# A sparse graph layer and a masked attention layer: rows put in order of their neighbour count on the chip

## The chip, the cores and the metric

The kernel runs on one core of a Trainium2 chip. The core has five engines that the text names by their short forms: PE (TensorE, matrix products), DVE (VectorE), ACT (ScalarE), POOL (GpSimd) and SP (SyncE, which only issues DMAs here). The time is that of the device, in microseconds (us): 2217.14 us for the kernel before, the median of 3 runs (2214.53 to 2218.22).

## The reference

`x` holds 8 graphs of 2048 rows with 256 features, and `adj` is one weighted 2048 x 2048 adjacency matrix that all graphs share. It is sparse: row `n` is linked to row `m` with a chance that falls as `1/sqrt((1+n)(1+m))`, so the first rows have many neighbours and the last ones few. Every row is linked to itself.

```
# layer 0: graph convolution, two linear layers with batch norm
A_norm = adj + eye;  deg = sum(A_norm, 0) + sum(A_norm, 1) - diag(A_norm)
agg = (A_norm * rsqrt(deg)[:, None] * rsqrt(deg)[None, :]) @ x
h   = relu(batchnorm(agg @ W1.T + b1));  y = batchnorm(h @ W2.T + b2)
x   = layernorm(x + y)
# layer 1: attention with 4 heads of 64, masked to the neighbours
q, k, v = split(x @ W)
o   = softmax(q k^T / 8 where adj != 0) v
x   = layernorm(x + o)
```

## The kernel before

The 2048 rows are cut into 16 blocks of 128 rows, one row to a partition. Block 0 holds the rows with the most neighbours and is worked on as a dense block; the others use lists of neighbours.

**The search** (`search_steps`, L214). For each row the kernel turns the non-zero places of its adjacency row into numbers that fall with the column (L219) and takes the eight largest at a time over all 2048 columns (MAX8, L223), striking out what it found (L226), in 2 to 4 rounds. `list_steps` (L231) then makes the list of block `t`: `LISTS[t] = (r, cap)` means that each row keeps its first `r` neighbours in `r` aligned slots ("tiles" of 128 rows with one neighbour each), and what is left over in the block is packed into `cap` further tiles, through one-hot matrices built on DVE (L262, L265) and products on PE (L272). All blocks have 132 tiles together, 40 of them such left-over tiles.

**Stage A, loading** (L387 to L439). The 16 blocks of `adj` are loaded into 16 buffers ("slots", `Slot`, 1 MB each, which every later stage up to the attention shares). ACT sums the rows, PE the columns, POOL takes the power of -1/2 (`rsqrt`, L136).

**Stage B, dense** (L444 to L467). `x` is loaded, scaled and written to `xs_d`, one DRAM row of 8 KB for each node with all 8 graphs. Blocks 0 and 1 (`DENSE = 2`) are multiplied as dense matrices while it passes (L454).

**Stage C, sparse** (L512 to L627). For each of the 116 tiles of blocks 2 to 15, POOL issues two gathers through an index list ("indirect DMA"[...]): 4 bytes from `adj` for the weights (`gather_value`, L311, 16 tiles ahead) and 8 KB a row from `xs_d` (L524, up to 8 tiles ahead). A tile is then added up on DVE (L593 for the first of a block, L597 for the others) or, with a diagonal or one-hot matrix as weights, on PE (L606). The rest of the search and of the lists runs between the tiles. A finished block is transposed (L371) and multiplied with W1 (L489), and the result goes to `h_d`.

**Stage D, second linear layer** (L636 to L785). 16 pairs of 512-column pieces go through a Strassen-like scheme with 7 products instead of 8; POOL makes its four differences for each pair (`form`, L685, L694).

**Stage E, attention** (L856 to L1342). Two graphs are worked on at once, so there are four passes over the 132 tiles. A pass is prepared by 8 `projection` units, which load `y` and `x`, normalise, and write keys with values (`kv_d`) and queries (`q_d`) to DRAM. The units of the first pass stand alone ("the run-in"); those of the following passes lie between the tiles of the pass before. For each tile POOL gathers keys and values (`kg`, L1192, ten tiles ahead), for a left-over tile also the queries (`qg`, L1198); DVE multiplies and sums (L1210, L1212), ACT takes the exponential (L1221), DVE or ACT weigh the values (L1241, L1236), PE adds up (L1252). `finish` (L1062) divides on DVE, `residual` (L1070) adds to `x` on POOL, and the row is normalised and stored by SP (L1106).

All order is written by hand: each engine takes its instructions in the order in which the program emits them, and `at(n, f, ...)` puts a step of a unit behind tile `n`. POOL's queue holds its arithmetic and all gathers, SP's the plain loads and stores.

## Time and profile before

| what | us |
|---|---|
| median of 3 runs | 2217.14 |
| the profiled execution, its own time | 2243.83 |
| its span, from the first to the last instruction | 2242.0 |
| stage A: loading, to the first product of stage B | 0 to 73 |
| stage B: dense | 73 to 187 |
| stage C: sparse, to the end of the W1 products | 187 to 622 |
| stage D: last W1 products, then the 16 pairs from 664 | 622 to 846 |
| stage E: run-in, to the first tile | 846 to 996 |
| stage E: four passes of 132 tiles | 996 to 2218 |
| end | 2218 to 2242 |

The stages are read from the chain of work that ended last and from the lists of instructions by time. In a row of a group of instructions, "busy" is the sum of the durations (overlaps counted once), then the mean of one in ns, then the time the engine stood idle just before them and what ended it. "issue" is idle time in which nothing the profile shows was waited for. In a table by stretches each engine has its busy time and its number of instructions, and then come the granted PE clock, the share of the 16 DMA engines and the rate of the DMAs.

### The profile page before, as it was taken

To read this page: it belongs to the slowest core of one execution; us is meant where nothing else is said; L and a number is where in the kernel's file an instruction comes from. 1 tells how busy PE (TensorE), PEld (TensorE's weight loads), DVE (VectorE), ACT (ScalarE), POOL (GpSimd) and SP (SyncE) were. 2 spreads that over 40 slices of the span, in tenths; PEclk is the share of its full clock that TensorE was granted. 3 is DMA by queue.
4 is the path that set the end of the run, shared out by engine and by line. 5 is a ranking of instruction groups with operands and counts; after the bars stand their busy time and mean duration, and the time that the engine had idled before them with its cause. 6 is when DMAs were issued, how large, how long until landed. Compare 5 with 4: busy or idle time off the path is not lost.

```text
span 2242.0 us, 27795 instructions
## 1 busy us (share of the span) xinstructions
PE 1989.4 (89%) x7720; PEld 1285.6 (57%) x7720; DVE 1824.6 (81%) x3461; ACT 1303.6 (58%) x3896; POOL 1445.7 (64%) x1443
## 2 busy tenths in 40 slices
PE   5899797899999997979999999999999999678884
PEld 1444344454444444647777777777777776566663
DVE  6897999798556663239999999899988999978996
ACT  6331132233354544647777777777777777678875
POOL 2504778886048771136777787768876778878884
PEclk7899898999999998989999999999999999889896
DMA  8887999899567625569898999999999999999994
GB/s 317 282 300 290 369 339 367 317 424 370 210 247 285 231 85 204 194 247 340 301 368 325 346 356 357 343 324 375 330 363 350 333 359 337 349 357 339 334 350 151
DMA packets 232628, 698.67 MB, mean 312 GB/s; under 512 B 24976, under 2 KB 91280, under 8 KB 206352
## 3 DMA queue, kind: packets, MB, share of 16 engines
q0 software_dynamic: 109248, 442.68, 52.9%
q1 hardware_dynamic: 120912, 237.34, 29.1%
q10 hardware_dynamic: 2304, 16.78, 1.8%
q8 instruction: 64, 1.05, 0.2%
q14 instruction: 100, 0.82, 0.1%
HBM read 565.91 MB, written 130.81 MB: 311 GB/s over the span
## 4 chain that ended last, share of the span: by engine, by line
PE 44%; DVE 26%; issue 9%; DMA 8%; ACT 7%; POOL 6%; another core or an unknown queue 0%; SPq 0%; DVEq 0%; POOLq 0%; ACTq 0%
PE pm L977 9%; PE pa L699 8%; PE po L1252 7%; DVE pr L1210 7%; PE pa L454 5%; PE ph L489 5%; DVE wv L1241 4%; ACT wv L1236 3%; DVE s L1212 3%; DMA e<-xs_d,idx 3%; POOL kg L1192 2%; PE pa L606 2%; DMA e<-in_adj_dram 2%; PE po L1045 2%; DVE e L597 2%
## 5 line engine op out<-in xcount | busy, mean ns | idle before, releaser
L1192 POOL DMA_INDIRECT kg<-kv_d,idx x528 | 567.6, 1075 | 159.4 <-issue 103.4
L1236 ACT ACTIVATE wv<-kg,pw 128x65 f32<-128x65 f32 x1896 | 477.6, 337 | 8.8 <-PE po L1045 3.8
L1252 PE MATMUL po<-wv,ident 128*128 128x260 f32 x1472 | 421.2, 399 | 51.4 <-DVE z L1066 39.1
L1212 DVE TENSOR_REDUCE s<-pr 128x8 f32<-128x512 f32 x528 | 362.1, 686 | 34.7 <-DVE pr L1210 0.5
L977 PE MATMUL pm<-wq,x1t 128*128 128x512 f32 (+1 forms) x1024 | 374.8, 496 | 12.6 <-ACT x1t L922 10.0
L1252 PEld LDWEIGHTS po<-wv,ident 128*128 128x128 f32 x1472 | 277.9, 198 | 122.2 <-issue 66.9
L1221 ACT ACTIVATE pw<-s,padb 128x8 f32<-128x8 f32 x528 | 157.2, 299 | 201.4 <-DVE s L1212 161.4
L1210 DVE TENSOR_TENSOR pr<-qb,kg 128x512 f32<-128x512 f32 x368 | 260.2, 707 | 4.0 <-issue 1.0
L977 PEld LDWEIGHTS pm<-wq,x1t 128*128 128x128 f32 x1024 | 186.1, 192 | 103.7 <-issue 73.7
L524 POOL DMA_INDIRECT e<-xs_d,idx x116 | 148.3, 1279 | 140.5 <-DMA xs_d<-xt 66.1
L1241 DVE TENSOR_TENSOR wv<-kg,pw 128x520 f32<-128x520 f32 x291 | 211.0, 725 | 16.8 <-PE po L1252 5.7
L1252 PE MATMUL po<-wv,oh 128*128 128x260 f32 x640 | 196.6, 398 | 7.8 <-DVE wv L1241 6.5
L489 PE MATMUL ph<-e,w1s 128*128 128x512 f32 x448 | 197.4, 593 | 0.0
L1198 POOL DMA_INDIRECT qg<-q_d,idxq x160 | 164.6, 1029 | 48.8 <-issue 47.9
L311 POOL DMA_INDIRECT av<-in_adj_dram,fidx x116 | 162.3, 1399 | 45.8 <-issue 32.3
L493 ACT ACTIVATE h<-ph,b1s 128x512 f32<-128x512 f32 x112 | 76.9, 687 | 181.1 <-PE ph L489 171.2
L606 PE MATMUL pa<-e,wt 128*128 128x512 f32 x352 | 166.9, 622 | 12.3 <-DVE wgt L323 4.6
L1045 PEld LDWEIGHTS po<-kvr,p 128*128 128x128 f32 x1024 | 138.9, 199 | 37.1 <-ACT p L1034 13.3
L1045 PE MATMUL po<-kvr,p 128*128 128x65 f32 x1024 | 136.0, 278 | 21.4 <-ACT p L1034 9.8
L1026 PE MATMUL pm<-q,kt 128*128 128x256 f32 x512 | 140.7, 400 | 13.1 <-POOL q L929 9.8
L597 DVE SCALAR_TENSOR_TENSOR e<-e,wgt,e 128x2048 f32<-128x2048 f32 x58 | 135.9, 2343 | 9.2 <-DMA e<-xs_d,idx 6.2
L1252 PEld LDWEIGHTS po<-wv,oh 128*128 128x128 f32 x640 | 120.4, 199 | 37.9 <-issue 15.8
(192 smaller groups left out, 3352.0 us busy)
## 6 DMA issues: line engine op xcount, KB each, us to landing
kv_d<-kvr SPq DMA_DIRECT2D x32, 1032.0 KB
h_d<-h SPq DMA_DIRECT2D x28, 1024.0 KB
e<-h_d SPq DMA_DIRECT2D x28, 1024.0 KB
e<-in_adj_dram SPq DMA_DIRECT2D x16, 1024.0 KB
xt<-in_x_dram SPq DMA_DIRECT2D x16, 1024.0 KB
xs_d<-xt ACTq DMA_DIRECT2D x16, 1024.0 KB
y_d<-y SPq DMA_DIRECT2D x32, 512.0 KB
yt<-y_d SPq DMA_DIRECT2D x32, 512.0 KB
```

What stands on the lines that cost most here:

```text
L489: nc.tensor.matmul(ph, w1s[:, d, f * P : (f + 1) * P], v[:, d, b, :], start=(d == 0), stop=(d == ND - 1),)
L597: nc.vector.scalar_tensor_tensor(agr[t].t, xg[n].t, wgt[:, col : col + 1], agr[t].t, op0=ALU.mult, op1=ALU.add,)
L606: nc.tensor.matmul(pa[c], w, xg[n].t[:, c * CH : (c + 1) * CH], start=(k == 0), stop=(k == count - 1),)
L699: nc.tensor.matmul(py, w[:, f, :], t[:, f, :], start=(f == 0), stop=(f == 1))
L977: nc.tensor.matmul(pm, x1t[b, c][:, d, i * P : (i + 1) * P], rhs(d), start=(d == 0), stop=(d == ND - 1),)
L1045: nc.tensor.matmul(po0[b][:, h, :], p[:, h, :], heads(kvr[b, c][:, i, D:])[:, h, :], start=(j == 0 and h == 0), stop=(j == NT - 1), skip_g ...
L1192: nc.gpsimd.indirect_dma_start(out=kg[n].rearrange("p b e -> p (b e)"), out_offset=None, in_=kv_d[p][:], in_offset=bass.IndirectOffsetOnAx ...
L1210: nc.vector.tensor_mul(pr, q, kg[n][:, :, :D])
L1212: nc.vector.tensor_reduce(s.rearrange("p b h -> p (b h)"), pr.rearrange("p b (h e) -> p (b h) e", e=HD), AX.X, ALU.add,)
L1236: nc.scalar.activation(wv[n][:, b, hs], k[:, b, D:][:, hs], AF.Copy, scale=w[:, b, h : h + 1],)
L1241: nc.vector.tensor_mul(wv[n].rearrange("p b (h e) -> p b h e", e=VW), k[:, :, D:].rearrange("p b (h e) -> p b h e", e=VW), w[:, :, :, None ...
L1252: nc.tensor.matmul(po[p, t, b].rearrange("p h e -> p (h e)"), oh[n] if e >= 0 else ident, wv[n][:, b, :], start=(r == 0), stop=(r == ELL[t ...
```

## The change

Each row's number of neighbours is counted, and the rows are ranked by it on the chip: rank 0 is the row with the most neighbours. Row `n` gets its place `pos[n]`; the 2048 places are again cut into 16 blocks. Rows of one block now have nearly the same number of neighbours, so block `t` has `DEPTH[t]` aligned tiles and no left-over tiles, and the last tiles of a block hold only the rows that still have a neighbour (`FEWER`, partial tiles of 4 to 120 rows). There are 125 tiles instead of 132 (14,988 rows instead of 16,896).

- **Search** (`search`): MAX8 runs on 16 segments of 8 to 248 columns and then on the 128 candidates. ACT counts neighbours (a second pass over each block). Ten blocks are searched before the ranking, six after it. The search is over before stage C.
- **Records**: a row's list, number, degree factor and count are written as one 128-byte record to its place in `rec_d` by an indirect DMA for each block (`hand_over`), and read back in order. `pos` is written to `pos_d`.
- **Dense**: only block 0 (the 128 rows with the most neighbours, gathered into `hubs`) is dense; block 1 is sparse as well. The tiles of a block are shared by DVE and PE as `ON_TENSOR` says (28 on PE, 97 on DVE).
- **Stage C**: before the first tile POOL issues 7 value gathers, 10 row gathers, 17 value gathers and `own_rows`. Between the tiles POOL also issues `lookups`: because keys and values are stored in order of rank, each of the 125 index lists is translated through `pos_d` by a 4-byte indirect DMA (62 in stage C, 32 in stage D, 31 in the run-in), and 16 scatters of the mask of block 0.
- **Stage E**: `x` rows are gathered by index (128 indirect DMAs on POOL instead of 32 loads on SP), output rows are scattered by index (128 indirect DMAs on POOL instead of 34 stores on SP), no queries are gathered and no one-hot tiles are made, and `finish` adds to `x` itself, in four instructions on DVE, so that `residual` is gone.

```diff
+DEPTH = (0, 19, 14, 12, 11, 9, 9, 8, 7, 7, 6, 6, 5, 5, 4, 3)
+GROUPS = ((0, 1, 8, 13), (2, 6, 12, 15), (3, 5, 10, 14), (4, 7, 9, 11))
+TURN = (0, 15, 14, 13, 1, 12, 2, 11, 3, 10, 4, 9, 5, 6, 7, 8)
+ON_TENSOR = (0, 6, 4, 3, 3, 2, 2, 2, 2, 2, 1, 1, 0, 0, 0, 0)
...
+    def search(t):
+        s = rows_of.pop(t)
+        a = s.t
+        nc.vector.scalar_tensor_tensor(a, a, 0.0, down, op0=ALU.not_equal, op1=ALU.mult)
+        best = lists.tile([P, 8 * (len(SEGMENTS) - 1)], F32, name="best", bufs=2)
+        for i, (u, v) in enumerate(zip(SEGMENTS, SEGMENTS[1:])):
+            nc.vector.max(out=best[:, 8 * i : 8 * i + 8], in_=a[:, u:v])
+        s.done()
+        for r in range(MAXNB // 8):
+            m8 = own[:, t, 8 * r : 8 * r + 8]
+            nc.vector.max(out=m8, in_=best)
+            if r + 1 < MAXNB // 8:
+                nc.vector.match_replace(out=best, in_to_replace=m8, in_values=best, imm_value=0.0)
...
+    def hand_over(t):
+        nc.vector.tensor_tensor(
+            own[:, t, MISS : MISS + 1], found[:, t : t + 1], count[:, t : t + 1],
+            op=ALU.not_equal,
+        )
+        spill(rec_d[:], posi[:, t : t + 1], own[:, t, :])
...
+                nc.scalar.activation(junk, a, AF.Sign, accum_out=count[:, t : t + 1])
...
+            for t in range(AHEAD_OF_RANK):
+                search(t)
...
+            nc.gpsimd.dma_start(pos_d.rearrange("(t p) o -> p (t o)", p=P), posi)
...
+            hubs = Slot()
+            pick(hubs.t, adj[:, :], hubi)
+            for t in range(AHEAD_OF_RANK, NT):
+                search(t)
+            for t in range(NT):
+                hand_over(t)
...
+        nc.sync.dma_start(rec, rec_d.rearrange("(t p) e -> p t e", p=P))
...
+        VLEAD, START = 24, 7
+        for n in range(START):
+            gather_value(n)
         gather_ahead(0)
+        for n in range(START, VLEAD):
+            gather_value(n)
+        own_rows = Slot()
+        pick(own_rows.t, xs_d[:], hubi)
+        nc.vector.scalar_tensor_tensor(
+            agr[0].t, own_rows.t, row_scale(0), agr[0].t, op0=ALU.mult, op1=ALU.add
+        )
...
         for n in range(len(tiles)):
...
+            v = n + VLEAD
+            if v < len(tiles):
+                gather_value(v)
...
+            if n % 2:
+                next(lookups, None)
+            if n % 7 == 3 and n // 7 < NT:
+                m = n // 7
+                spill(bias_d[:], posi[:, m : m + 1], masks[:, m, :])
...
             gather_ahead(n + 1)
...
             second_linear(n)
+            for _ in range(2):
+                next(lookups, None)
...
+            def load_rows(b, c, i):
+                t = GROUPS[c][i]
+                pick(x1[b, c][:, i, :], x_rows, idr[:, b, t : t + 1])
...
             def finish(b, t, po):
+                c, i = place[t]
                 ri = inv_all[:, b, t, :]
                 nc.vector.reciprocal(ri, po[:, :, HD])
-                z = zs[b, t] = ip.tile([P, D], F32, name="z", bufs=4)
-                nc.vector.tensor_mul(
-                    heads(z), po[:, :, :HD], ri[:, :, None].to_broadcast([P, NHEADS, HD])
-                )
-
-            def residual(b, t):
-                c, i = divmod(t, TPC)
-                to = rest[b] if late(b, t) else x1[b, c]
-                nc.gpsimd.tensor_add(to[:, i, :], zs.pop((b, t)), to[:, i, :])
+                to = heads((rest[b] if late(b, t) else x1[b, c])[:, i, :])
+                for h in range(NHEADS):
+                    nc.vector.scalar_tensor_tensor(
+                        to[:, h, :], po[:, h, :HD], ri[:, h : h + 1], to[:, h, :],
+                        op0=ALU.mult, op1=ALU.add,
+                    )
...
+            def put(b, c, i):
+                t = GROUPS[c][i]
+                spill(out_rows, idr[:, b, t : t + 1], x1[b, c][:, i, :])
...
             for n in range(min(later), 0):
                 side_tasks(n)
+                next(lookups, None)
```

`pick` is an indirect DMA that gathers rows by an index list, `spill` one that scatters them; both are issued by POOL.

## The prediction

> **What bounds the kernel now.** I read the stretches first, one for each stage (stage E at one pass), to see who is busy in each.
>
> ```profile
> core 0: us, PE busy (x) PEld busy (x) DVE busy (x) ACT busy (x) POOL busy (x), PEclk, DMA share, GB/s
> 73.00:187.00 114.00, 112.66 (x257) 49.61 (x258) 97.25 (x77) 28.78 (x17) 29.09 (x28) 0.98 0.83 290
> 187.00:272.00 85.00, 73.57 (x222) 36.04 (x223) 83.99 (x133) 10.31 (x23) 59.09 (x48) 0.97 0.87 346
> 272.00:450.00 178.00, 156.47 (x442) 78.28 (x441) 156.37 (x318) 45.58 (x71) 137.98 (x97) 0.91 0.90 339
> 450.00:622.00 172.00, 166.57 (x486) 80.64 (x484) 135.04 (x232) 59.11 (x93) 83.19 (x59) 0.98 0.81 327
> 664.00:846.00 182.00, 180.56 (x421) 79.73 (x420) 118.02 (x174) 81.81 (x119) 138.76 (x60) 1.00 0.52 196
> 846.00:963.00 117.00, 101.62 (x392) 64.76 (x392) 34.86 (x108) 67.82 (x162) 14.13 (x56) 0.93 0.56 191
> ...
> 1301.00:1606.00 305.00, 285.00 (x1356) 218.99 (x1355) 283.40 (x587) 230.33 (x789) 232.22 (x264) 0.98 0.94 347
> ```
>
> PE fills stages B and D. Stage C is held by DVE up to 272 (84 of 85 us, search and lists) and then by PE. In a pass of stage E, PE and DVE share the limit, 285 and 283 of 305 us. POOL looks free. The second view, the groups, says what one piece of its work costs.
>
> ```profile
> L1192 POOL DMA_INDIRECT kg<-kv_d,idx x528 | 567.6, 1075 | 159.4 <-issue 103.4
> L524 POOL DMA_INDIRECT e<-xs_d,idx x116 | 148.3, 1279 | 140.5 <-DMA xs_d<-xt 66.1
> L1198 POOL DMA_INDIRECT qg<-q_d,idxq x160 | 164.6, 1029 | 48.8 <-issue 47.9
> L311 POOL DMA_INDIRECT av<-in_adj_dram,fidx x116 | 162.3, 1399 | 45.8 <-issue 32.3
> L489 PE MATMUL ph<-e,w1s 128*128 128x512 f32 x448 | 197.4, 593 | 0.0
> L606 PE MATMUL pa<-e,wt 128*128 128x512 f32 x352 | 166.9, 622 | 12.3 <-DVE wgt L323 4.6
> L597 DVE SCALAR_TENSOR_TENSOR e<-e,wgt,e 128x2048 f32<-128x2048 f32 x58 | 135.9, 2343 | 9.2 <-DMA e<-xs_d,idx 6.2
> ```
>
> A 4-byte gather costs POOL no less than one of 8 KB a row. Why their means differ from the commonest duration, 0.94 us, shows in order of time:
>
> ```profile
> 199.30 2.29 DVE L223 MAX8 nbx<-e 128x8 f32<-128x2048 f32 x1
> ...
> 200.50 0.93 POOL L524 DMA_INDIRECT e<-xs_d,idx  x1 [0.30 <-issue]
> ...
> 324.52 2.34 DVE L597 SCALAR_TENSOR_TENSOR e<-e,wgt,e 128x2048 f32<-128x2048 f32 x1
> 324.95 2.73 POOL L311 DMA_INDIRECT av<-in_adj_dram,fidx  x1 [0.30 <-issue]
> ...
> 327.99 0.94 POOL L524 DMA_INDIRECT e<-xs_d,idx  x1 [0.30 <-issue]
> 329.14 2.34 DVE L597 SCALAR_TENSOR_TENSOR e<-e,wgt,e 128x2048 f32<-128x2048 f32 x1
> 329.23 3.07 POOL L311 DMA_INDIRECT av<-in_adj_dram,fidx  x1 [0.31 <-issue]
> ```
>
> A gather that starts under a multiply-add of DVE ends 0.82 us after it (326.86 to 327.68, 331.48 to 332.30); one under MAX8 is not held. With 0.30 us of issue behind each, a gather occupies POOL 1.24 us, plus what it is held.
>
> **Before the sparse stage.** ACT reads each block twice: its 2.45 us per block become 4.45, so the counts end near 5.9+71 = 77. A search is one pass (2.29, L219), 16 MAX8 over 2048 columns in all (2.13 by the 2.29 row; 0.06 to 0.16 more for each, I take 0.11: 3.9) and 1.9 for the 128 candidates: 8.1 us. Ten, from 10.4 on, end at 91. Ranking and its round trips to PE and POOL, some 13, the list of hubs, 9 (16 products at 0.55): 113. POOL's plain DMA of 4-byte places stands ahead of the degree factor; from 1 us to 15 (2048 descriptors at POOL's 0.94 for 128), I take 2, in the 13. Six searches, 49: 162. Then POOL has 16 records, 20 us: 182; landing, reading back and index arithmetic 8: **190** (175 to 205). One dense block, 128 products of 0.44 = 56 us on PE, from about 123 to 179, and the passage of `x` lie under this. So the list is ready when stage C begins now, and stages A and B gain nothing: what leaves stage C (search and one-hot lists on DVE) goes ahead of it.
>
> **The sparse stage.** DVE: 15 first tiles at 1.28, 82 multiply-adds at 2.3, 11 blocks of `add_rows` (44 at 0.74), 120 statistics at 0.69, small ones 10: some 335 us. PE: 28 tiles of 3.44, 480 W1 products of 0.43, transposes 32: 335. At the 0.93 that PE and DVE reach elsewhere that is 360, against 435 now. But POOL:
> - At the opening, 35 indirect DMAs before and with `own_rows`: 43 us, and its landing 4. DVE waits for it; the weights and all multiply-adds are queued behind that, and PE's transposes and ACT's diagonal matrices wait for those. Start: **238**.
> - Then up to the last row gather: 101 values, 57 lookups, 16 masks, 115 rows = 289 at 1.24 = 358 us.
> - Held: now 39.8+52.7 us beyond 0.94 in the two groups, over some 70 two-input passes (58 of L597, 12 of the search), 1.3 each with POOL occupied 77% of the time, so 1.7 at full occupation (2.34 less half a gather is 1.72; back to back it is 1.1). I take 1.6 for 74 of them: 118.
> - Partial tiles: 18 with 72 rows on average. The trace has none; their cost lies between no saving and one in proportion (0.41 x 45 = 18). I take 9.
>
> Here the GPSIMD Engine Reference of the Trainium skill (Key points) goes further than the row: contention comes from DVE instructions with two SBUF inputs, which the rows show, *and* from those in a 2-port mode. The first-tile pass (1.28 us for 2048) is such a one; no gather starts under one here, so the rule would add up to 14 x 0.65 = 9 us. I leave it out, as the rows are silent.
>
> Sum 467 from 233: the last row gather at 700, last tile and transposes 15, last W1 products 14 (32 x 0.435, half of now), run-in of stage D 21.5 as now: its pairs start at 751 instead of 664, **+87**.
>
> **Second linear layer.** POOL has 4 x 2.36 a pair and 2 lookups, 11.9 us against PE's 11.2; over 14 pairs it falls back 10, of which its lead covers about half: **+5** (0 to 12). The 512-byte stores of `y` go to DMA engines half idle: 0.
>
> **Run-in.** POOL, almost idle now, takes 4 row gathers a unit and a lookup at every step, and the degree root that ACT waits for is queued behind them. Until the 31 lookups end, a unit takes 10 x 1.24+1.5 = 13.9 instead of 12.1, and 18 DMAs stand before the first root: 872 instead of 860. The fifth root comes at 923 instead of 905: **+18** (5 to 25).
>
> **Four passes.** For each: seven tiles fewer save DVE 7 x (1.38+0.44) = 13 and 12 of one-hots; four divisions at 0.13 to 0.23 instead of one of 0.42 cost 3 to 16, I take 10: -15. PE: 28 products of 0.4: -11. POOL: 125+64 indirect DMAs at 1.34, roots 25, 3 more: 281 us, as now (232 busy and 47 of issue), for `residual` and `qg` pay for the rows and outputs. In a pass of 294 that is 96%. A store waits for ACT's apply, and the gathers behind it wait too; ten tiles of lead cover that. SP loses the 8 loads and some 8 stores that move to POOL and issues 4 pieces where it stored keys and queries in one; nothing waits for it now. The transfers fall by 18 MB a pass; DVE hardly waits for them, so 0. I take **-8 a pass, -32** (0 to -48). Covered if POOL keeps up; if not, the gain is gone.
>
> **Sum:** 87+5+18-32 = +78 on the profiled 2243.83: 2322. The runs' median is 1.2% lower; I put the difference on it: 2217+78 = **2295**.
>
> **Rivals.**
> 1. *POOL's holds are hidden*: if PE and DVE, at 360 from 238, set stage C, POOL's 358 fit in, and pairs start near 656: -8+5+18-32, **2200**. For: gathers run ten ahead, and the trace now has POOL idle in stage C. Against: these are the same gathers, a third more of them for a tile. It decides at a hold of 0.55 us per multiply-add; above it the kernel is slower.
> 2. *POOL bounds the passes too*: gain gone, 10 more of waits for stores: **2340**. For: 96%. Against: it gets fewer bytes and no `residual`.
> 3. *The opening is quicker than I sum* (segments at 7.2 a search, records read by 175) and short tiles cost in proportion, with holds of 1.1: -15-9-37: 2234.
> The change may not do what it says: 500 tiles instead of 528 are certain, but if short tiles cost as full ones, only the 9 us above is lost.
>
> **Chances.** Forecast 0.48 (2260 to 2335), first rival 0.24, second 0.18, third 0.10. Below 0.2% (4 us) a run of this kernel tells no change: its three lie within 0.17%. Slower 0.72, same 0.04, faster 0.24, where the third rival gives the middle. From 2190 to 2345 half of the first rival and a third of the second are left out.
>
> **What would show it.** POOL's stretches of stage C full (busy and issue over 95%), PE and DVE with waits for `e<-xs_d`; gathers ending 0.82 after multiply-adds; a hole in PE before the first transpose; in the run-in ACT waiting for the root. Wrong if stage C's tiles follow each other at 2.9 us, or if the passes gain over 15 us each.

## The result and the profile after

The changed kernel takes **2421.60 us** (median of 4 runs, 2420.71 to 2424.01), the kernel before 2217.68 us beside it (4 runs, 2214.53 to 2220.63): 1.092 times as long, 95% interval 1.0903 to 1.0940. The forecast was 2295 with a range of 2190 to 2345. The direction was right, and the time lies 77 us above the range.

The profiled execution of the changed kernel took 2421.29 us with a span of 2419.6, so it stands at its median. The first profiled execution of the kernel before did not: 2243.83, 26 above its median. I therefore profiled the kernel before once more (e9 below): 2220.35 us, span 2218.6. The two agree to 3 us in all stages but one: the four passes took 1219.4 us in the first and 1199.2 in the second. The second is the measure from here on.

| stretch, and the mark that ends it | before (second profile) | after | difference | forecast |
|---|---|---|---|---|
| A to C, up to the first copy of stage D | 652.1 | 810.4 | **+158.3** | +87 |
| D, up to the first batch norm of a `y` tile | 199.2 | 195.6 | -3.6 | +5 |
| run-in, up to the first product of a tile's scores | 142.5 | 165.5 | **+23.0** | +18 |
| the four passes, up to the last such product | 1199.2 | 1225.3 | **+26.1** | -32 |
| end | 25.6 | 22.8 | -2.8 | 0 |
| span | 2218.6 | 2419.6 | +201.0 | +78 |

The stretches of the changed kernel, by engine, with the granted PE clock, the share of the DMA engines and the rate in the last three columns:

```profile
core 0: us, PE busy (x) PEld busy (x) DVE busy (x) ACT busy (x) POOL busy (x), PEclk, DMA share, GB/s
149.00:205.00 56.00, 26.75 (x63) 11.57 (x61) 3.37 (x19) 5.66 (x5) 15.55 (x16) 0.79 0.30 112
205.00:270.00 65.00, 0.00 (x0) 0.00 (x0) 4.80 (x17) 0.19 (x1) 38.43 (x40) 0.50 0.58 187
270.00:520.00 250.00, 182.51 (x467) 86.33 (x468) 154.26 (x146) 62.09 (x105) 196.25 (x138) 0.84 0.75 257
520.00:780.00 260.00, 191.63 (x469) 88.01 (x468) 160.76 (x155) 58.89 (x100) 212.29 (x156) 0.86 0.84 294
823.00:1004.00 181.00, 178.00 (x415) 78.46 (x413) 118.71 (x175) 81.55 (x118) 166.65 (x92) 1.00 0.59 185
1301.00:1606.00 305.00, 285.99 (x1358) 216.12 (x1357) 275.22 (x630) 225.65 (x771) 219.64 (x248) 0.98 0.87 291
```

From 149 to 270 us little runs but POOL: DVE is busy for 8 of 121 us, and PE stands still for the whole of 205 to 270, where its granted clock is 0.50. In the sparse stage, 270 to 780, PE (374 of 510 us) and DVE (315) both have gaps. POOL is busy for 409, and its 294 instructions, all but four of them DMAs, have 0.30 us of issue before each, 87 more: 496 of 510. It is the fullest engine of this stage, as the forecast had it; whether it is the bound, e1, e2 and e14 test. In the passes DVE is busy for 275 of 305 us, where the kernel before had 283 with more tiles to do: no engine is full there (PE 286, DVE 275).

The groups that answer to those shown of the kernel before:

```profile
L126 POOL DMA_INDIRECT kg<-kv_d,idk x500 | 528.2, 1056 | 166.1 <-issue 80.9
L626 DVE SCALAR_TENSOR_TENSOR e<-e,wgt,e 128x2048 f32<-128x2048 f32 (+8 forms) x82 | 192.3, 2346 | 127.4 <-DMA e<-xs_d,idx 126.9
L132 POOL DMA_INDIRECT out_dram<-x,idr x126 | 138.9, 1103 | 129.8 <-DMA out_dram<-x,idr 67.1
L126 POOL DMA_INDIRECT av<-in_adj_dram,fidx x125 | 167.3, 1339 | 68.1 <-issue 29.9
L634 PE MATMUL pa<-e,wt 128*128 128x512 f32 x224 | 137.0, 768 | 84.9 <-DMA e<-xs_d,idx 84.9
L126 POOL DMA_INDIRECT e<-xs_d,idx x125 | 171.4, 1371 | 39.9 <-issue 30.5
L126 POOL DMA_INDIRECT idk<-pos_d,idx x125 | 142.7, 1141 | 35.2 <-issue 32.7
```

Multiply-adds and products now wait for row gathers, 126.9 us on DVE and 84.9 on PE (6.2 and 4.3 before). The line that the forecast did not have is the third: an output store by index waits on POOL for the output store before it, 67.1 us in all. What is queued behind it waits too, here the key gathers (start, duration, engine, line, and in brackets the idle time before it and what ended it):

```profile
2067.90 0.94 POOL L126 DMA_INDIRECT kg<-kv_d,idk  x1 [0.30 <-DVE inv_all L1083]
2072.07 1.01 POOL L132 DMA_INDIRECT out_dram<-x,idr  x1 [3.23 <-DMA out_dram<-x,idr]
2073.38 0.94 POOL L126 DMA_INDIRECT kg<-kv_d,idk  x1 [0.30 <-issue]
2078.01 1.18 POOL L132 DMA_INDIRECT out_dram<-x,idr  x1 [3.68 <-DMA out_dram<-x,idr]
2079.49 1.44 POOL L126 DMA_INDIRECT kg<-kv_d,idk  x1 [0.30 <-issue]
```

Three stretches of POOL in order of time show where the 158 us begin. First, the records:

```profile
149.22 1.03 POOL L132 DMA_INDIRECT rec_d<-own,posi  x1 [41.69 <-DVE own L246]
155.54 0.98 POOL L132 DMA_INDIRECT rec_d<-own,posi  x1 [5.29 <-DMA rec_d<-own,posi]
158.40 0.97 POOL L132 DMA_INDIRECT rec_d<-own,posi  x1 [1.88 <-DMA rec_d<-own,posi]
161.88 0.96 POOL L132 DMA_INDIRECT rec_d<-own,posi  x1 [2.51 <-DMA rec_d<-own,posi]
```

Each scatter into `rec_d` starts only when the one before has landed, 1.88 us of idleness and more behind 0.97 of work, so 16 of them take from 149.2 to 199.3. The wait is part of the program: before all but the first of these scatters POOL executes a semaphore wait (a semaphore is a counter that a DMA raises when it has landed), and the records of the trace name the semaphore of the scatter before. The kernel's source asks for no such wait; it came in where the program was built.

```profile
L132 POOLq EVENT_SEMAPHORE  x15: 17/17/2357, 154.8 to 197.7; - x15
```

Then the opening, where the row gathers of 1 MB each are still on their way:

```profile
229.22 0.94 POOL L126 DMA_INDIRECT av<-in_adj_dram,fidx  x1 [1.97 <-DMA e<-xs_d,idx]
231.46 0.95 POOL L126 DMA_INDIRECT av<-in_adj_dram,fidx  x1 [1.30 <-DMA e<-xs_d,idx]
...
238.49 0.94 POOL L126 DMA_INDIRECT av<-in_adj_dram,fidx  x1 [3.60 <-DMA e<-xs_d,idx]
243.13 1.10 POOL L126 DMA_INDIRECT av<-in_adj_dram,fidx  x1 [3.71 <-DMA e<-xs_d,idx]
```

A value gather needs none of these rows, and yet it is let go only when one of them has landed. The trace's records name the semaphores here too: POOL's DMAs use eight of them in turn, and a DMA waits until the one eight places before it, which has the same semaphore, has landed. Here that is a row gather of 1 MB. And the loop:

```profile
399.49 2.35 DVE L626 SCALAR_TENSOR_TENSOR e<-e,wgt,e 128x2048 f32<-128x2048 f32 x1
400.57 2.08 POOL L126 DMA_INDIRECT idk<-pos_d,idx  x1 [0.30 <-issue]
402.95 2.33 DVE L626 SCALAR_TENSOR_TENSOR e<-e,wgt,e 128x2048 f32<-128x2048 f32 x1
402.96 0.94 POOL L126 DMA_INDIRECT e<-xs_d,idx  x1 [0.30 <-issue]
404.21 1.90 POOL L126 DMA_INDIRECT av<-in_adj_dram,fidx  x1 [0.31 <-issue]
```

The lookup that starts under a multiply-add ends 0.81 us behind it (401.84 to 402.65), the value gather 0.83 behind the next (405.28 to 406.11). The gather at 402.96, which starts with the multiply-add, is not held. The pass over a block's first tile (1.28 us, one input) does the same:

```profile
315.31 1.26 DVE L623 TENSOR_SCALAR e<-e,wgt 128x2048 f32<-128x2048 f32 x1
315.47 1.92 POOL L126 DMA_INDIRECT av<-in_adj_dram,fidx  x1 [0.30 <-issue]
```

Here too the gather ends 0.82 us behind DVE (316.57 to 317.39). The profile of before shows it as well, at four places which the prediction overlooked when it wrote that no gather starts under one. The first of them, with the gather's end at 394.72, 0.84 behind DVE:

```profile
392.60 1.28 DVE L593 TENSOR_SCALAR e<-e,wgt 128x2048 f32<-128x2048 f32 x1
392.92 1.80 POOL L524 DMA_INDIRECT e<-xs_d,idx  x1 [0.30 <-DVE wgt L305]
```

### The profile page after: what moved, and what is told of

Read it like the earlier page. It is cut to its first block, busy times and chain, and to the rows that moved or that the text cites. A ratio compares the mean times of both kernels' runs of the same rounds, so it can differ in the third digit from the quotient of the medians.

```text
span 2419.6 us, 27604 instructions
## 1 busy us (share of the span) xinstructions
PE 1912.3 (79%) x7262; PEld 1222.5 (51%) x7262; DVE 1718.1 (71%) x3584; ACT 1308.9 (54%) x3823; POOL 1615.1 (67%) x1601
## 5 line engine op out<-in xcount | busy, mean ns | idle before, releaser
L126 POOL DMA_INDIRECT kg<-kv_d,idk x500 | 528.2, 1056 | 166.1 <-issue 80.9
L1275 PE MATMUL po<-wv,ident 128*128 128x260 f32 (+6 forms) x2000 | 560.1, 409 | 64.0 <-DVE x L1086 46.0
L1275 PEld LDWEIGHTS po<-wv,ident 128*128 128x128 f32 (+6 forms) x2000 | 378.4, 201 | 189.7 <-issue 100.6
L1258 ACT ACTIVATE wv<-kg,pw 128x65 f32<-128x65 f32 (+7 forms) x1800 | 453.4, 337 | 4.3 <-ACT pw L1246 3.8
L1234 DVE TENSOR_TENSOR pr<-qb,kg 128x512 f32<-128x512 f32 (+7 forms) x500 | 339.8, 680 | 60.9 <-DMA kg<-kv_d,idk 58.1
L1236 DVE TENSOR_REDUCE s<-pr 128x8 f32<-128x512 f32 (+7 forms) x500 | 342.6, 685 | 33.5 <-ACT pw L1246 0.7
L626 DVE SCALAR_TENSOR_TENSOR e<-e,wgt,e 128x2048 f32<-128x2048 f32 (+8 forms) x82 | 192.3, 2346 | 127.4 <-DMA e<-xs_d,idx 126.9
L1246 ACT ACTIVATE pw<-s,padb 128x8 f32<-128x8 f32 (+7 forms) x500 | 147.6, 298 | 224.2 <-DVE s L1236 223.4
L132 POOL DMA_INDIRECT out_dram<-x,idr x126 | 138.9, 1103 | 129.8 <-DMA out_dram<-x,idr 67.1
L634 PE MATMUL pa<-e,wt 128*128 128x512 f32 x224 | 137.0, 768 | 84.9 <-DMA e<-xs_d,idx 84.9
L1263 DVE TENSOR_TENSOR wv<-kg,pw 128x520 f32<-128x520 f32 (+2 forms) x275 | 189.7, 690 | 14.1 <-PE po L1275 6.6
L126 POOL DMA_INDIRECT idk<-pos_d,idx x125 | 142.7, 1141 | 35.2 <-issue 32.7
```

Source lines behind the costliest of these rows:

```text
L126: nc.gpsimd.indirect_dma_start(out=out, out_offset=None, in_=table, in_offset=bass.IndirectOffsetOnAxis(ap=index, axis=0),)
L626: nc.vector.scalar_tensor_tensor(a, xg[n].t[:here], w, a, op0=ALU.mult, op1=ALU.add)
L1234: nc.vector.tensor_mul(pr[:k], qb[p, t][:k], kg[n][:k, :, :D])
L1236: nc.vector.tensor_reduce(s[:k].rearrange("p b h -> p (b h)"), pr[:k].rearrange("p b (h e) -> p (b h) e", e=HD), AX.X, ALU.add,)
L1246: nc.scalar.activation(pw[n][:k], sc.pop(n)[:k], AF.Exp, bias=padb[:k, t, r : r + 1])
L1258: nc.scalar.activation(z[:, b, hs], k[:, b, D:][:, hs], AF.Copy, scale=w[:, b, h : h + 1],)
```

## The experiments

The theory after the result (theory 1): the sparse stage takes as long as POOL's queue does, so every indirect DMA in it costs its 1.24 us, every multiply-add on DVE its hold; and in the passes the indexed stores cost by what they make POOL wait, since the key gathers stand behind them. The rivals: the late start of DVE sets the end of the stage; PE or the transfers would set it anyway; the passes lose their gain to something other than the stores.

A note on comparing. The marks up to the end of stage D repeat within about 5 us wherever the unchanged kernel or one with changes only behind them ran (stage C's last multiply-add starts at 776 to 781), so those stages are compared across chips. The passes are not: e1 to e4 ran on a chip where the kernel before took 2250 us, e13 to e15 on the same one, where it then took 2242; the passes of every variant profiled there were longer. Passes are therefore compared only inside e5 to e7 (before: 2218) and e16 to e18 (before: 2214), each on one chip. For the same reason the whole times of e1, e2 and e3 (2454.6, 2521.1 and 2535.8 us) say nothing against the sums of whole kernels that were expected of them; their stages do.

### e1, the lookups taken away

```diff
+        nc.vector.tensor_copy(idk, key)
...
-    lookups = lookup_steps()
+    lookups = iter(())
```

> The 125 translations through pos_d are left out; keys and values are gathered by the untranslated numbers, as many gathers as before, so the output is not the reference's. Changed kernel: 2421.6 us. Theory 1 (POOL's throughput sets stage C): 62 indirect DMAs fewer at 1.24 and 0.46 held each take 105 us from stage C (516 to about 411), and the run-in loses its 19 us: about 2297. Theory 2 (rows land late: transfer time or the gate at the opening set stage C, POOL merely looks busy): stage C stays within 20 us, and only the run-in gains: 2385 to 2405.

The last multiply-add starts at 713.0 instead of 779.5: **-66**, between the 105 of the first theory and the under 20 of the second. That is POOL's queue, but less than one price a DMA. The groups of POOL within its sparse stage say why:

```profile
L126 POOL DMA_INDIRECT e<-xs_d,idx x112 | 169.7, 1515 | 46.3 <-issue 25.6 <-PE ph L312 10.0 <-DMA e<-xs_d,idx 4.6
L126 POOL DMA_INDIRECT av<-in_adj_dram,fidx x98 | 141.7, 1446 | 31.3 <-issue 26.6 <-DMA av<-in_adj_dram,fidx 2.5 <-DMA e<-xs_d,idx 1.5
L132 POOL DMA_INDIRECT bias_d<-masks,posi x16 | 24.3, 1521 | 4.9 <-issue 4.9
```

Beyond 0.94 us each, these 226 DMAs were held 336-212 = 123 us; in the unchanged kernel, 288 DMAs of the same stretch were held 131. Fewer DMAs are held for about as long: the hold goes with the multiply-adds, not with the gathers. So 61 lookups are worth 61 x 1.24 = 76 and not 105; 10 us went to waits for a buffer that PE had not yet freed. The run-in, too, was shorter: 149 us, where e2 and e3 on the same chip had 173 and 176.

### e2, twenty multiply-adds moved from DVE to PE

```diff
-ON_TENSOR = (0, 6, 4, 3, 3, 2, 2, 2, 2, 2, 1, 1, 0, 0, 0, 0)
+ON_TENSOR = (0, 9, 6, 5, 5, 4, 4, 3, 3, 3, 2, 2, 2, 0, 0, 0)
```

> ON_TENSOR raised from 28 to 48 tiles, so that 20 multiply-adds with two SBUF inputs leave DVE and PE gets 20 x 3.44 = 69 us more (379 to 448 us in stage C). Same number of indirect DMAs. Theory 1 with holds (POOL is held by DVE's two-input passes, 1.6 us each): stage C 32 us shorter, about 2390. Theory 1 without holds (only the count of DMAs matters) and theory 2: no change, 2415 to 2425. If PE is nearer to its limit than it looks: slower.

The last multiply-add starts at 758.8, **-21** where 32 were expected. POOL was held for 373-272 = 101 us over 289 DMAs, 30 less than 131, which is 1.5 us for each multiply-add that left; part of it came back as waits of POOL for buffers that PE still read (12.0 us where there was 0.3). With 62 multiply-adds 101 us, with 82 of them 131, and 123 in e1: 1.5 to 1.6 each in all three, the first-tile passes included.

### e3, the hub rows gathered first

```diff
+        own_rows = Slot()
+        pick(own_rows.t, xs_d[:], hubi)
+        nc.vector.scalar_tensor_tensor(
+            agr[0].t, own_rows.t, row_scale(0), agr[0].t, op0=ALU.mult, op1=ALU.add
+        )
...
         for n in range(START):
             gather_value(n)
         gather_ahead(0)
```

> own_rows is gathered first of all in stage C, so that DVE and PE can start about 45 us earlier; POOL's number of DMAs is unchanged. If the gate at the opening costs what DVE and PE stand idle there (60 us of wait for own_rows): about 45 us less, 2377. If POOL's queue sets the end of stage C whatever DVE does at its start: 0 to 15 us less, 2406 to 2422.

DVE passes `own_rows` at 211 instead of 268 and begins the multiply-adds 43 us earlier, at 230.0. The last of them starts at 785.5, **6 us later**. So the wait at the opening, the longest single one on DVE (60.2 us), costs nothing by itself: the rows that DVE would work on are still to be gathered, and POOL's queue is as long as before.

### e12, e13: the records stored without an index

```diff
-        spill(rec_d[:], posi[:, t : t + 1], own[:, t, :])
+        nc.sync.dma_start(rec_d[t * P : (t + 1) * P, :], own[:, t, :])
```

> The changed kernel with the 16 blocks of records stored plainly by SP instead of by index; the lists are then in the unsorted order, so short tiles leave neighbours out and the output isn't the reference's; sizes and numbers of all later instructions are the same. In the changed kernel POOL starts the 16 scatters at 149 us, 2.87 us from one to the next, and the first value gather at 205. Theory (each scatter waits for the landing of the one before, and what comes after moves with POOL's start): the records are written by 155, fidx is done at 170 or so instead of 204.6, and the end of the multiply-adds moves with it, from 779 to 743 to 750. Rival (the dense block and the passage of x set the start of stage C, the xs rows being ready only by 180 to 185): first row gathers wait for xs_d and the end falls by less than 20.

This missed. The list was done 34 us later, at 239.1, because the 16 stores stood on SP ahead of the loads of `x` and held them until the last search was over:

```profile
SPq L250 <- DVE own L246: 104.0, 2, 103.6
```

It still says one thing: the list came 34 us later and the last multiply-add 37 us later (816.5), about one for one. The second attempt leaves the stores on POOL (`nc.gpsimd.dma_start` in the same line):

> The records stored plainly again, but from POOL's queue, where the scatters were, so that SP's loads of x don't stand behind them. (Lists unsorted: the program finds more neighbours than its tiles have room for and at the end of its own accord runs its long path, so that only the stages before it can be compared.) Theory: no wait from store to store, 16 x 1.2 to 1.4 us in a row from 149 on, the list at 178 to 182 instead of 204.6, and the last multiply-add as much earlier, 779 to 753 to 757, D at 784 to 788. Rival (the dense block and the passage of x end only by 200 and set the start): list and D within 8 us of the changed kernel's 204.6 and 810.

```profile
149.13 5.18 POOL L250 DMA_DIRECT2D rec_d<-own  x8 [41.70 <-DVE own L246]
154.69 0.54 POOL L250 DMA_DIRECT2D rec_d<-own  x1 [0.38 <-issue]
155.75 3.71 POOL L250 DMA_DIRECT2D rec_d<-own  x7 [0.52 <-DMA rec_d<-own]
```

Sixteen stores in 10.3 us instead of 50.1. The list is done at 170.7, **34 us earlier**, the last multiply-add at 741.6, 38 earlier, and D begins 36 earlier (774.3): more than the 22 to 26 expected, since a store took 0.65 us and not 1.2 to 1.4. Nothing else was in the way of the start. The places of these stores are known when the program is built, and in the trace's records none of them waits for the one before; each waits at most for the DMA eight before it. (In e12, e13 and e14 the rows stay unsorted; the program then takes its own long path at the end, 14.3 to 14.6 ms in all, so that only the earlier stages count.)

### e14, the three reliefs at once

The edits of e1, e2 and e13 together.

> The three reliefs of POOL at once: plain records from POOL, no lookups (the keys are then fetched by the unsorted index, and the output isn't the reference's), 20 multiply-adds handed to PE. Alone they moved the end of stage C by 26 (expected of the run before), 66 and 21 us. Theory (POOL's queue is the whole of the stage's loss, and its parts add up): D starts at 690 to 710, within 60 us of the kernel before (652). Rival (with POOL relieved twice, PE at its low granted clock or the transfers set the end): 725 or later.

D begins at 690.6 instead of 810.4: **-120**. By the same mark e1 had gained 65, e2 17 and e13 36, together 118. The parts add up, and what is left is another bound:

```profile
270.00:400.00 130.00, 125.93 (x323) 58.88 (x324) 80.80 (x80) 35.84 (x64) 93.32 (x73) 0.96 0.92 318
400.00:530.00 130.00, 119.15 (x319) 55.79 (x318) 80.17 (x86) 35.57 (x65) 102.28 (x78) 0.96 0.94 340
530.00:656.00 126.00, 125.78 (x347) 59.53 (x346) 82.73 (x88) 38.87 (x71) 82.67 (x65) 1.00 0.95 363
```

PE is busy for 371 of 386 us and the DMA engines for 92 to 95%; POOL, with its issue, for 343. So POOL was the bound of the changed kernel's sparse stage, and behind it, 120 us away, stand PE, which here has 20 tiles more than in the changed kernel, and the transfers. Even then the stage ends 38 us later than in the kernel before; no run takes these away.

### e4, e15: outputs stored plainly

```diff
-                spill(out_rows, idr[:, b, t : t + 1], x1[b, c][:, i, :])
+                nc.sync.dma_start(out[b, t * P : (t + 1) * P, :], x1[b, c][:, i, :])
```

> The 128 scatters of output rows become plain stores on SP, a block in its sorted place, so the output is in the wrong row order. If a scatter that waits for the one before it (67 us of POOL's waits) delays the key gathers behind it: DVE's 58 us of waits for kg go, the four passes fall from 1225 to about 1190, 2385. If POOL's lead of ten tiles covers these waits and the passes are held by PE and DVE: under 8 us, 2414 to 2422.

> Plain stores of the outputs by SP, in the sorted order, once more: on the first chip, where the kernel before took 2250 us, this variant's passes took 1209 and those of three variants with indexed stores 1321 to 1333; on the chip of the four tables, where it took 2218, indexed stores took 1227 and four tables 1167. Theory (a plain store frees POOL of the wait just as four tables do, and the first chip adds some 40 us to either): where the kernel before takes about 2218, the passes come to 1160 to 1175. Rival (plain stores gain less than four tables because SP's transfers then fall together with its own loads): 1200 to 1215 here too.

The passes took 1209 and 1196 us, on the chip on which e1, e2 and e3 had 1321 to 1333, e13 1316 and e14 1298. That looks like a gain of some 100 us, but there was no kernel on that chip that differed in the stores alone, so it settled nothing by itself. e15 was meant for a chip on which the kernel before takes 2218 us and came on this one, so that its two cases could not be told apart.

### e5, e6, e7: what in the passes costs

e5 is the changed kernel again. In e6 the outputs of three of the four groups of blocks go to scratch tables (`out_t`, each of the output's size), a table for each of a group's four blocks, so that four such stores in a row have four targets. The fourth group (`c == NCH - 1`) still stores into the output. (What was expected of e6 describes this as three of each group's four outputs; the edit is as said here.)

```diff
-                spill(out_rows, idr[:, b, t : t + 1], x1[b, c][:, i, :])
+                table = out_rows if c == NCH - 1 else out_t[i][:]
+                spill(table, idr[:, b, t : t + 1], x1[b, c][:, i, :])
```

> The changed kernel itself, as the measure of the next two runs on this chip. Both theories: up to the first run-in of a y tile at 1006 us the marks stay within 5 us (multiply-adds 273 to 780, D pairs near 823). The passes were 1225 us in its first profile and 1321 to 1333 in the three variants with indexed stores. Theory 1 (what the indexed stores cost is the wait of each for the one before, and this wait depends on the chip or on the run): the passes fall on either value, and the wait of out_dram for out_dram goes with it. Rival (the three variants lost it by their own changes): 1225 again.

> Three of each group's four output tiles go by index to three scratch tables of the output's size instead of to the output, which stays incomplete; so four indexed stores in a row have four targets. As many instructions on POOL, as many bytes. Theory 1 (a store into the table into which another is under way waits for its landing, 1.5 to 4 us, and holds the key gathers that are queued behind it): the waits of out_dram for out_dram (67 us in the first profile) all but vanish and the passes come to 1210 plus or minus 10, as with plain stores. Rival (the 126 instructions on POOL cost it, 139 us and 38 of issue): the passes stay within 10 us of the unchanged kernel's on this chip.

The passes take 1227.1 us in e5 and **1167.3** in e6, with the same number of instructions on POOL. The two groups of stores in e6:

```profile
L134 POOL DMA_INDIRECT out_t<-x,idr x94 | 106.0, 1127 | 27.9 <-issue 21.7 <-ACT pw L1249 2.4 <-DMA kg<-kv_d,idk 1.5
...
L134 POOL DMA_INDIRECT out_dram<-x,idr x32 | 35.1, 1097 | 28.1 <-DMA out_dram<-x,idr 10.7 <-issue 6.8 <-ACT x L869 5.0
```

141 us of work as before; of the 66.1 us of store waiting for store in e5, 10.7 are left, in the group that still has one target. 55 us less waiting made the passes 60 us shorter, more than the expected 1210, which had been taken from the plain stores on the slower chip.

In e7 the rows of `x` are loaded by SP, and 128 indirect DMAs leave POOL:

```diff
-                pick(x1[b, c][:, i, :], x_rows, idr[:, b, t : t + 1])
+                nc.sync.dma_start(x1[b, c][:, i, :], x[b, t * P : (t + 1) * P, :])
```

> The rows of x for the residual are loaded by SP as plain 128-row blocks instead of by index (they are then in the unsorted order, and the output isn't the reference's); 128 indirect DMAs leave POOL. Run-in, from the first y tile to the first score: my sum has four of these in each unit of 13.9 us, without them ACT's 12.1 sets the pitch, so 165 falls to 148 (145 to 152). Passes: if POOL's total of instructions set them, they fall by 40 or more (84 x 1.3 = 110 us out of POOL); if the waits of the indexed stores do, by less than 15.

The run-in falls to **142.0**, the 142.5 of the kernel before: its loss is the row gathers and lookups in front of the degree roots, as forecast. The passes fall by 18, to 1209.4, between my two numbers. POOL had about 110 us less to do, but the stores now waited 104.8 us for one another instead of 66.1: part of the relief was spent waiting at the next store.

### e16, e17, e18: one target, four targets, plain stores on one chip

The kernels of e5, e6 and e4 once more, together.

> The changed kernel, as the measure for the next two on one chip. Passes 1225 to 1230 where the kernel before takes about 2218, 1300 to 1330 where it takes 2242 or more (so far only variants of it were seen there).

> Four targets for the indexed stores, on the same chip as the last and the next run. Theory (waiting is what the indexed stores cost): 55 to 65 us less in the passes than the unchanged kernel, on a slow chip too. Rival (on the slow chip something else adds about 100 us to every kernel with indexed stores): there they stay above 1260.

> Plain stores of the outputs in the sorted order, same chip. Theory (plain stores and four tables do the same): passes within 10 us of the four tables' here. Rival (indexed stores cost something of their own on the chip, beyond the wait): plain stores are faster than four tables by 30 us or more. Third case (plain stores gain less, SP's queue holds them up): slower than four tables by 30 or more.

The passes: **1225.9, 1170.4, 1135.3** us (whole kernels: 2420.7, 2364.4, 2336.0). What DVE waits for in the passes moves the same way. Below are the waits of its first instruction for a tile (total, times, longest), in the first profile after, then with four targets (e17), with plain stores (e18), and in the kernel before (e9):

```profile
DVE pr L1234 <- DMA kg<-kv_d,idk: 58.1, 50, 4.2
```
```profile
DVE pr L1237 <- DMA kg<-kv_d,idk: 22.9, 23, 3.8
```
```profile
DVE pr L1234 <- DMA kg<-kv_d,idk: 2.3, 3, 1.0
```
```profile
DVE pr L1210 <- DMA kg<-kv_d,idx: 3.2, 6, 0.8
```

The key gathers come late by the stores ahead of them on POOL. Four targets take away the wait of store for store, 55 us; putting the stores on SP takes another 35. Of the cases written down for e18, the second held: indexed stores cost something beyond the wait for one another. What remains of them on POOL in e17 is 141 us of work and 58 of idle time before it; which part of this makes the 35, no run separates. With no store in its way, the sorted order does shorten the passes, by 64 us against the kernel before (1199.2, on another chip, where it takes 3 us more).

On the chip with a kernel before of 2242 to 2250 us, plain stores took 60 to 75 us more and indexed stores 70 to 107 more than here. Its traces show waits of ACT and DVE, 73 to 173 us in all, that end with a signal for which the profile has no instruction ("remote"). The runs on the other chips have none, except the first profile of the kernel before, the one that took 26 us more, with 20 us. What delays these signals is left open.

### e8, e10, e11: the search in segments alone, in the kernel before

One part of the change in the old kernel: MAX8 on 16 segments, then 2 to 4 rounds on the 128 candidates. The sum of the numbers found is compared with the sum that the first pass accumulates, so that a row with more than eight in a segment is noticed.

```diff
-            for r in range(ROUNDS[t]):
-                m8 = nbx[:, t, 8 * r : 8 * r + 8]
-                nc.vector.max(out=m8, in_=a)
...
+            for i, (u, v) in enumerate(zip(SEGMENTS, SEGMENTS[1:])):
+                nc.vector.max(out=best[:, 8 * i : 8 * i + 8], in_=a[:, u:v])
...
+            for r in range(ROUNDS[t]):
+                m8 = nbx[:, t, 8 * r : 8 * r + 8]
+                nc.vector.max(out=m8, in_=best)
```

> The kernel before with the search in segments alone (16 MAX8 over pieces, then the rounds over 128 candidates; the sum of what was found is compared with the sum of the row, so that a miss is flagged), everything else as before, the search done in the dense stage. DVE loses 15 x (12.2 - 7.5) = 70 us, and of the stretch 187 to 272, which DVE held with 84 of 85 us busy, the 27 search steps of 2.29, 62 us. Theory: PE then sets stage C, which has 397 us of PE in the 435 us: 25 to 39 us less, so 2185 to 2195 where the kernel before takes 2217. Rival (the lists, one step a tile, or the row gathers set the opening): less than 10 us.

**2202.49 us** (4 runs, 2200.48 to 2204.47) against 2218.14 (7 runs, 2215.97 to 2220.87): 0.9932 times, 95% interval 0.9915 to 0.9948. That is 0.7%, a small gain but clear of the spread, and faster than both kernels of this case. D begins at 633.4 instead of 652.1, 19 us earlier, less than the 25 to 39 expected. The opening of the sparse stage and the stretch behind it, in e8:

```profile
187.00:272.00 85.00, 85.00 (x253) 41.77 (x252) 43.00 (x123) 14.04 (x30) 55.24 (x48) 1.00 0.94 371
272.00:450.00 178.00, 156.38 (x453) 77.85 (x452) 155.70 (x344) 47.33 (x74) 142.56 (x100) 0.93 0.93 365
```

In the opening DVE falls from 84 to 43 of 85 us and PE rises from 74 to 85, the 11 us that were to be had there. In the second stretch nothing changes: PE and DVE at 156 of 178, as in the kernel before.

Moving tiles of blocks 1 to 3 from PE to the idle DVE looked like the next step:

```diff
-        return 3 if t < 4 else ELL[t]
+        return 5 if t < 4 else ELL[t]
```

> The kernel before with the segmented search (2202.5 us), and of the blocks 1 to 3 five tiles each instead of three on DVE: 6 tiles leave PE. In the segmented kernel PE is busy for all of 187 to 272 and DVE for 43 of these 85 us. Theory (PE alone sets this stretch): 4 tiles of 4 x 0.43 us there, 7 us, and 3 more in block 1 at the end: 2193 to 2197. Rival (the multiply-adds hold up the gathers on POOL, 1.6 us each, and the order of the row gathers sets the stretch): within 3 us of 2202.

> As the last one, with seven tiles on DVE in the blocks 1 to 3, 12 fewer on PE. Theory: 14 us in the opening if DVE, then at 62 of 71 us, keeps up, 5 more at the end: 2184 to 2192. Rival: DVE and POOL's held gathers take the lead, 2200 or more.

2205.44 us (0.9935, interval 0.9913 to 0.9956) and 2201.65 (0.9914, 0.9888 to 0.9939): no difference from e8, and neither of the gains expected. With seven tiles, PE fell to 63 of 85 us in the opening, and its transposes waited for DVE's finished block for 27.3 us instead of 12.8. My sum for it was a share of busy time; the order (sums on DVE, then transposes, then W1 on PE) spent it.

### e9, the kernel before again

> The kernel before itself, for a second profile. Its first profiled execution took 2243.83 us, 26 more than the median of its runs, and the changed kernel's equals its median, so the comparison stage by stage has these 26 us in it. Theory 1 (they lie in the passes, where its first profile has 1219 us and the kernel with the segmented search, with the same passes, 1196): here passes near 1196 and a span near 2216. Rival (they lie in stages A to C, or every profile of it has them): passes near 1219 and a span near 2240.

Passes 1199.2, span 2218.6: theory 1. Of the 23 us between the two profiled executions, 20 lie in the passes.

## Why the prediction was right and wrong

Two steps of the prediction failed, and both left out the same wait, that of an indexed store for the landing of the one before: "POOL has 16 records, 20 us" took 50, and "ten tiles of lead cover that" was not so, for DVE waited 58 us for keys. A third wait, for semaphores that POOL's DMAs share, added 26 us of POOL's time to stage C. The path through POOL was right.

**The bound of the sparse stage: right.** POOL, with its holds, sets it (e1, e2, e14), and the first rival (holds hidden) is refuted. Stage D cost nothing, where +5 was forecast: PE is busy for 178 of 181 us in it. The hold was nearly sized right: 131 to 133 us instead of 118. I had 1.6 us for 74 multiply-adds; it was about 1.5 for all 82, and 11 us for the 15 first-tile passes. Those I had left out, "as the rows are silent", which was a misreading of the trace, against the rule of the GPSIMD Engine Reference of the Trainium skill (Key points) that DVE's instructions in a 2-port mode contend with POOL too; the estimate from it was 9 us. The holds under these passes agree with the rule; that they run in such a mode was taken from their 1.28 us, and no run shows the mode itself.

**The size of stage C: +158 instead of +87.** The 71 us lie in three terms of the sum.
- *The list ready at 190.* It was ready at 204.6. The searches ended sooner than I had summed (149 instead of 162: 7.42 us a block instead of 8.1). But "POOL has 16 records, 20 us" took 50, because each scatter into `rec_d` waits for the one before. e13 priced this wait: 34 us of the kernel's time. I had costed the issue and left out the order of two writes into one table. A price for the landing could have been had: the page DMA: Bandwidth & Descriptors of the Trainium skill (Anatomy of one DMA, SWDGE path) gives a DMA from POOL about 2.0 us of fixed time whatever its size. The trace agrees roughly: the scatters landed 2.1 us after their start at the least and 2.4 in the median, and up to 5.6.
- *The opening, "35 indirect DMAs, 43 us".* It took 57 (205.5 to 262.8): 35 x 1.24, and 14 of waiting for row gathers that had the same semaphores. DVE's start at 268 instead of 238 was its consequence and, by e3, of no weight in itself. That POOL's 14 us are, follows from the queue as the bound; no run took them away alone.
- *The loop, 467 us.* From 262.8 to the end of the last row gather on POOL, 769.5, it took 507: 290 DMAs x 1.24 = 360 (358), held 133 (118), and 14 of waits, 12 of them again for a row gather with the same semaphore. For short tiles (17 of them with 68 rows on average, not 18 with 72) I had taken 9 off; the lookups of the run-in, one of them with 4 rows, took 0.90 to 1.19 us, and most of them 0.94 to 0.95, as with 128. There is nothing to take off.

**Run-in: right**, +23 for +18, and by its mechanism (e7: without the row gathers 142.0).

**The passes: +26 instead of -32.** I wrote "a store waits for ACT's apply, and the gathers behind it wait too; ten tiles of lead cover that". What the stores waited for ACT was less (some 42 us in the profile's list of waits); the store also waits for the store before it, 67 us, and the lead did not cover it: DVE waited 58 us for keys. With four targets, and so nearly without this wait, the passes take 1167 to 1170 us, 29 to 32 below the kernel before. That this is the gain forecast is luck: the gain on DVE and PE had been put too low, for with the stores off POOL it is 64 (e18), and the indexed stores cost more than their wait. "If POOL keeps up" was named as the condition, and the second rival had the gain gone; what it lacked was that POOL can fall behind while idle, by waiting.

**The base.** I put the 26 us between profile and median on everything alike. By e9 nearly all of it belonged to the passes, so that the forecast -32 started from a stage that normally has 1199 us and not 1219.

Added up: 71 (stage C) + 58 (passes) + 5 (run-in) - 9 (D) - 3 (end) = 122 us too little, of the 127 between 2295 and 2422; the rest is profile against median.

**Where the gain of the change went.** Its DVE work was saved: the search alone is worth 16 us (e8), the sorted passes up to 64. It was paid for on POOL: records, lookups and part of the holds 120 us in stage C (e14), row gathers 23 in the run-in (e7), stores 91 in the passes (e18). The other 38 us of stage C stay unexplained in part: e14 shows PE and the transfers full there, but not what a kernel with fewer tiles on PE would take.

## What to carry to other kernels

When plain transfers become indexed ones, cost them as a queue: count every indirect DMA at its full turn on the issuing engine whatever its size (here 1.24 us, 4 bytes or 8 KB a row, 4 rows or 128), add the hold by what DVE runs beside it, and then ask which two of them write the same tensor: in the program here each of these waited for the other's landing and held whatever was queued behind. Several target tensors took nearly all of this wait away. Look also at how many of the engine's DMAs the program lets be under way; here a DMA could wait for the one eight places before it. An engine that is about 70% busy (POOL in the passes, 220 of 305 us) can hold up the others through such waits. And look for the part of a change that pays by itself: here the search in segments, which needed none of the sorting.

## What the runs showed of the hardware

- Indexed stores into one DRAM tensor went one at a time: 2.85 us from one to the next in `rec_d` at best, against 0.65 for plain stores of the same blocks from the same engine (16 in 10.3 us). Spread over four tensors, the output stores hardly waited for one another (10.7 us instead of 66.1). The wait is put there by the program and not by the queue: it is a semaphore wait of POOL before the store, for the store before.
- At the opening POOL's indirect DMAs of 512 bytes started only when a gather of 1 MB had landed with which they have nothing to do (1.1 to 3.7 us each). This too is the program's: all of its 1166 DMAs from POOL share eight semaphores in turn, and one waits, where it must, for the one eight places before.
- The hold of POOL's DMAs goes by the passes of DVE and not by the DMAs: 131 us for 82 multiply-adds with 288 DMAs, 123 for 82 with 226, 101 for 62 with 289. A DMA that starts under such a pass ends about 0.82 us behind it, and so it does under the one-input pass of 1.28 us.
- The kernel before took 2214 to 2218 us (medians) on three of the chips and in the first comparison, and 2242 and 2250 on another; the passes with many indexed stores differed more than that (70 to 107 us).
